# A decoder's first layer: weights loaded ahead of the mask, ternary weights made during attention, causal scores begun as the mask, ten steps for eleven

## The chip, the cores and the metric

The kernel runs on one core of a Trainium2 chip. The metric is device time in microseconds (us) of one execution, the median of several runs. A core has five engines with a queue of instructions each: PE (TensorE, matmuls and transposes; its weight loads are shown apart as PEld), DVE (VectorE), ACT (ScalarE), POOL (GpSimd) and SP (SyncE, which here only issues DMAs). DMAs are issued from the queues of SP, ACT and POOL, and each issuer has a DMA queue of its own, served by the same 16 DMA engines.

## The reference

A decoder of four layers, each of self-attention, cross-attention to a context and a feed-forward part (ffn), on 8 sequences of 128 tokens with 256 features, all in f32. The change touches layer 0 alone:

```python
x = x + _L0_attn_ref(_layernorm(x), Wq, bq, Wk, bk, Wv, bv, Wp, bp)      # 16 heads of 16, causal
x = x + _L0_xattn_ref(_layernorm(x), ctx_1024, pos, pos, Wq, Wkv, Wout, bout)  # 32 heads of 8
x = x + _L0_ffn_ref(_layernorm(x), gate_w, gate_b, val_w, val_b, out_w, out_b) # 1024 hidden
...
def bit_linear(x, w, b):                       # the three matmuls of layer 0's ffn
    gamma_x = clip(max(abs(x), axis=-1), 1e-05)
    x_dq = clip(round(x * 127 / gamma_x), -128, 127) * gamma_x / 127
    gamma_w = clip(mean(abs(w)), 1e-05)
    w_dq = clip(round(w / gamma_w), -1, 1) * gamma_w
    return einsum('bsd,hd->bsh', x_dq, w_dq) + b
```

So the ffn's weights become ternary (-1, 0 or 1 times the mean magnitude of the whole matrix), and each row of activations is rounded to 255 steps of its own largest magnitude. The ffn is `bit_linear(silu(bit_linear(x, gate)) * bit_linear(x, val), out)`.

## The kernel before, in words

Tokens lie on the 128 partitions, one sequence (128 tokens) at a time; x stays in SBUF for the whole kernel. Where a matmul needs features on partitions, PE transposes (`norm_turned`, L186 to L191). A planner puts the instructions of each stage in an order per engine by their dependences and due times; inside `manual_schedule` (`in_step`, L384) the order is the one written.

*Start* (`decoder`, from L2446; 0 to 25 us). SP loads the constants. ACT's queue loads x in two halves (L2459) and, behind them, the context cx (L2480), which PE transposes into ctxT first of all. POOL makes a table less_own_rows (L2498, a tensor_scalar of 16x2048) in a short-lived pool "start" and writes it to DRAM as less_own (L2501). A second short-lived pool "mask" holds the mask mu, loaded by a DMA on POOL's queue (L2510); DVE makes mb and anyk of it (L2513 to L2515). The pool wp0, in which the weights w, their rows r and the streamed blocks st have two buffers each (`weights` L101 and L107, `stream` L137), is opened after these two, in the place that they leave.

*Self-attention* (`l0_attn`, 25 to 130 us). PE makes Q, K (L46, into qT and kb) and V (into va) for all 1024 tokens. Meanwhile POOL adds the projection's bias to x (L184, 8 adds). Then a loop, by hand, over eight sequences, in which step t does parts of sequences t, t-1, ... with lags 0 to 3, so eleven steps. For a sequence: 16 score matmuls into the one buffer "sc" of four PSUM banks (L209); DVE adds the causal mask (L280, constant of 0 and -1e30) and copies into s in SBUF; DVE takes the row maxima (L285); POOL subtracts them (L286); ACT takes the exponentials in place (L301); PE turns the probabilities four times (L345), ACT copies each (L347), PE multiplies by the values; ACT copies the sum out (L367), PE turns it back (L375), DVE divides (L312, L316), PE projects, DVE adds to x (L195). At sequence 2 of `score` the kernel calls `clear_rows` (L1014): POOL issues one DMA of 8.4 MB that fills rows_in, a DRAM table which layer 1's ffn uses, with zeros.

*Cross-attention* (`l0_xattn`, 130 to 278 us): a prelude of projections and a rotary embedding, then a loop by hand of 16 units (two halves of the heads for each sequence), with four s buffers and four os buffers.

*ffn* (`l0_ffn`, 278 to 383 us). Front, to the first gate at 309.76: for each of three weights of 128x2048, DVE sums the magnitudes (L599), makes the mean (L602, L603, over a matmul with ones), and rounds it in three passes (L604 to L606) to bf16 wb. The loads of the first two lie in the two st buffers since the start of the kernel, and DVE made their sums at 32.80; the third is loaded when a buffer comes free. Then x is normalized (L618 to L624), the rows' maxima are taken (L632), xq is made in three passes (L640 to L642), and PE turns it (L648). Loop over eight sequences: gate and value matmuls in bf16, DVE scales and adds bias (L658, L663), ACT applies SiLU (L659), POOL multiplies (L664), DVE takes the row maximum (L667), rounds h in three passes (L673 to L675) to hq, PE turns it (L679), multiplies by the third weight, DVE adds to x (L683). Adding and subtracting the constant MAGIC = 1.5 * 2^23 rounds an f32 to an integer.

*Folds* (`folds`, L748 on): a generator of twelve pieces that make weights of later layers out of the inputs. A piece loads fold_vo on SP (L783, L784; two buffers), PE turns it (L769), ACT copies (L770), PE multiplies (L46), ACT copies out to fold_out (L775; two buffers) and SP writes that to DRAM (L776). Four pieces stand before the ffn's x work in the program, one in each step of the loop.

Of the kernel before, what the change touches and what calls it, by code (L numbers as in the profile page):

```python
# [8 lines left out]
F32 = mybir.dt.float32  # L9
BF16 = mybir.dt.bfloat16  # L10
# [187 lines left out]
def tok(b):  # L198
    return slice(b * S, (b + 1) * S)
# [24 lines left out]
def l0_attn(k):  # L224
# [7 lines left out]
    with k.tc.tile_pool(name="l0a", bufs=2) as wk_:  # L232
# [9 lines left out]
        for g in range(2):  # L242
            ts_ = slice(g * 512, (g + 1) * 512)
            for o in range(NC):
# [10 lines left out]
                )  # L255
        for b in range(B):
# [10 lines left out]
        caus = k.c[:, C_CAUS : C_CAUS + P].unsqueeze(1).to_broadcast([P, H, P])  # L267
        k.banks({"tr": 2, "po": 1, "o": 1})
        S_, PO, OS, PB, OB, PY = {}, {}, {}, {}, {}, {}
        act = nc.scalar.copy  # L270

        def score(b):
            if b == 2:
                clear_rows(k)
            psc = k.sct()
            for o in range(NC):
                scores(k, lambda r, n: psc[:, r, o * 256 : o * 256 + n], qT[:, o, tok(b)], kb[:, o, :, tok(b)])
            s = S_[b] = wk_.tile([P, 4, 4, P], F32, name="s", bufs=4)
            sv = s.rearrange("p r g t -> p (r g) t")
            nc.vector.tensor_tensor(sv, psc.rearrange("p r (g t) -> p (r g) t", t=P), caus, ALU.add)  # L280

        def less_max(b):
            sv = S_[b].rearrange("p r g t -> p (r g) t")
            mx = k.sm.tile([P, H], F32, name="mx")
            nc.vector.tensor_reduce(mx, sv, AX.X, ALU.max)  # L285
            nc.gpsimd.tensor_tensor(sv, sv, mx.unsqueeze(2).to_broadcast([P, H, P]), ALU.subtract)  # L286

        def values(b):
            po = PO[b] = k.pot()

            def use(g, pT):
                for r in range(4):
                    nc.tensor.matmul(
                        po[32 * r : 32 * r + 32, g, :], va[:, b, g, r, :], pT[:, r, :], start=True, stop=True
                    )

            round_about(k, wk_, lambda g: S_[b][:, :, g, :], [act] * 4, use)

        def exp(b):
            sf = S_[b].rearrange("p r g t -> p (r g t)")  # L300
            nc.scalar.activation(sf, sf, AF.Exp, scale=HD**-0.5)  # L301
# [21 lines left out]
        def project(b):  # L323
# [8 lines left out]
            (3, copied), (3, turn), (0, score), (3, divided), (0, less_max),  # L332
            (2, values), (1, exp), (3, project), (3, lambda b: k.add_x(b, PY[b])),
        )


def round_about(k, wk_, src, copies, use):


    done = {}  # L340
    for g in range(6):
        if g < 4:
            pt = k.trt()
            for r in range(4):
                k.nc.tensor.transpose(pt[:, r, :], src(g)[:, r, :], k.ident)  # L345
            done[g] = wk_.tile([P, 4, P], F32, name="pT", bufs=3)
            copies[g](done[g], pt)  # L347
        if g >= 2:
            use(g - 2, done[g - 2])
# [14 lines left out]
def back(k, wk_, po):  # L364

    os_ = wk_.tile([P, 4, P], F32, name="os", bufs=4)
    k.nc.scalar.copy(os_, po)  # L367
    return os_
# [19 lines left out]
def l0_xattn(k):  # L388
# [7 lines left out]
    with k.tc.tile_pool(name="l0x", bufs=2) as wk_, ExitStack() as inner:  # L396
# [104 lines left out]
        def score(u):  # L501
# [3 lines left out]
            s = S_[u] = wk_.tile([P, 4, 4, P], F32, name="s", bufs=4)  # L505
# [38 lines left out]
        def copied(b):  # L544
            OS[b] = back(k, wk_, PO[b])
# [36 lines left out]

def l0_ffn(k):
# [6 lines left out]
    with k.tc.tile_pool(name="l0f", bufs=2) as wk_:  # L590
        pieces = folds(k, wk_)
        wb = wk_.tile([P, 3, 2048], BF16, name="wb", bufs=1)
        gam = k.sm.tile([P, 3], F32, name="gam")
        rgam = k.sm.tile([P, 3], F32, name="rgam")
        part = k.sm.tile([P, 3], F32, name="part")
        for m in range(3):
            w = k.stream(a["p2"][m])[:, 0:2048]
            gm, rm = gam[:, m : m + 1], rgam[:, m : m + 1]
# [11 lines left out]
        for _ in range(4):  # L610
            next(pieces)
# [2125 lines left out]
```

## Time and profile before

| | us |
|---|---|
| median of three runs | 1948.71 |
| lowest and highest of them | 1945.85, 1960.44 |
| the profiled execution, its own time | 1957.12 |
| its span | 1955.3 |
| granted TensorE clock over the span | 0.939 |
| Q, K, V of layer 0 | 25.47 to 49.20 |
| layer 0's attention loop | 49.20 to 130.30 |
| its cross-attention, prelude and loop | 130.30 to 277.90 |
| its ffn, front and loop | 277.90 to 382.50 |

The profile is of one execution. Its page lists the busy time of each engine, the costliest groups of instructions (a line number is that of the kernel file, with output <- inputs, shape, count, busy time, mean of one in ns, and the idle time of the engine before them with what ended it), the chain of waits that ended last, and the DMA queues. A row of the timeline is: start, duration, engine, line, operation, output <- inputs, shape, count and, in brackets, how long its engine had been idle and what released it; "PEq", "SPq" and the like are the issue of a DMA by that engine's queue. A row of the DMA view is: queue, packets, MB, share of 16 engines' time; q1 is SP's queue, q10 ACT's, q0 POOL's. Some rows of the attention loop, for 49.2 to 130.3 us:

```profile
L286 POOL TENSOR_TENSOR s<-s,mx 128x2048 f32<-128x2048 f32 x8 | 28.9, 3611 | 47.0 <-DVE mx L285 33.6 <-ACT s L301 13.4
L280 DVE TENSOR_TENSOR s<-ps_sc,consts 128x2048 f32<-128x2048 f32 x8 | 18.3, 2287 | 11.8 <-PE ps_sc L209 11.8
L285 DVE TENSOR_REDUCE mx<-s 128x16 f32<-128x2048 f32 x8 | 18.2, 2280 | 0.2
L347 ACT COPY pT<-ps_tr 128x512 f32<-128x512 f32 x32 | 18.3, 587 | 26.9 <-PE ps_tr L345 26.9
```

DVE's two passes over a sequence's scores take 2.29 and 2.28, POOL's 3.61.

### The profile page before, as it was taken

Reading aid. Unit: us, or ns where it says so; the run is one execution under the profiler, and the core shown is the slowest. Engines: PE = TensorE matmul, PEld = TensorE weight load, DVE = VectorE, ACT = ScalarE, POOL = GpSimd, SP = SyncE. Lnnn points to the kernel's source line nnn. Section 1 sums busy time; section 2 is a strip of 40 time slices with the busy share of each in tenths; the row PEclk is TensorE's granted clock in tenths of the full one; section 3 lists DMA queues with packets and bytes.
Section 4 is the critical chain, followed back from the end, with each engine's and each line's share of the span. In section 5 each row is a group of like instructions: output and inputs, shape, how many; then the busy total and the mean of one; then the engine's idle time right before and its main releaser. Section 6 shows DMA issues by size and latency. Waiting matters only on the chain.

```text
span 1955.3 us, 25181 instructions
## 1 busy us (share of the span) xinstructions
PE 1717.8 (88%) x9471; PEld 1136.2 (58%) x9477; DVE 1203.0 (62%) x2374; ACT 1037.7 (53%) x1711; POOL 365.8 (19%) x359
## 2 busy tenths in 40 slices
PE   5776977667999986998788989999999997999999
PEld 3453655444666653664466545555555556888667
DVE  4766778856677752326756767677676775454423
ACT  2445854434667741225464377778777763343432
POOL 3543542201121222332002000000000001333200
PEclk9896988878999997998999999999999998999989
DMA  4600026305000022111001110101101004000000
GB/s 135 177 25 1 2 97 209 111 1 215 1 12 6 12 82 105 50 41 51 17 1 36 17 50 18 33 18 34 34 18 34 18 1 162 1 1 1 1 1 22
DMA packets 38970, 90.29 MB, mean 46 GB/s; under 512 B 6865, under 2 KB 19490, under 8 KB 37186
## 3 DMA queue, kind: packets, MB, share of 16 engines
q1 hardware_dynamic: 31266, 69.43, 10.4%
q0 software_dynamic: 5488, 17.67, 3.0%
q8 instruction: 76, 1.25, 0.3%
q10 hardware_dynamic: 2096, 1.57, 0.3%
q14 instruction: 44, 0.36, 0.1%
HBM read 67.15 MB, written 21.51 MB: 45 GB/s over the span
## 4 chain that ended last, share of the span: by engine, by line
PE 68%; DVE 14%; ACT 11%; issue 3%; POOL 2%; DMA 1%; ACTq 0%; DVEq 0%; SPq 0%; POOLq 0%
PE ps_xz L46 9%; PE ps_o L46 7%; PE ps_o L2077 6%; PE ps_o L848 5%; PE ps_mm L46 5%; PE ps_q L46 5%; PE ps_h L46 4%; PE ps_u L46 3%; PE ps_sc L46 3%; PE ps_y L46 2%; PE ps_ty L46 2%; PE ps_xz L1994 2%; DVE mx L511 2%; PE ps_ty L2015 2%; PE ps_sc L209 2%
## 5 line engine op out<-in xcount | busy, mean ns | idle before, releaser
L46 PE MATMUL ps_xz<-xnT,wxz 128*128 128x512 f32 x512 | 237.1, 607 | 0.3 <-ACT ee L1997 0.3
L46 PEld LDWEIGHTS ps_xz<-xnT,wxz 128*128 128x128 f32 x512 | 93.3, 192 | 103.9 <-issue 101.9
L1974 DVE SCALAR_TENSOR_TENSOR xc<-pad,w,xc 128x1024 f32<-128x1024 f32 x96 | 123.1, 1282 | 30.5 <-ACT xc L1968 28.7
L2077 PE MATMUL ps_o<-wo,yg 128*128 128x256 f32 x512 | 128.0, 395 | 1.5 <-DVE yg L2056 1.5
L848 PE MATMUL ps_o<-wvo,uT 128*128 128x256 f32 x512 | 122.6, 383 | 0.0
L848 PEld LDWEIGHTS ps_o<-wvo,uT 128*128 128x128 f32 x512 | 98.5, 193 | 40.7 <-issue 30.3
L1997 ACT ACTIVATE ee<-ps_xz,sgn 128x512 f32<-128x512 f32 x128 | 87.1, 689 | 60.2 <-PE ps_xz L1994 60.2
L2077 PEld LDWEIGHTS ps_o<-wo,yg 128*128 128x128 f32 x512 | 93.5, 192 | 25.4 <-issue 12.9
L2017 DVE TENSOR_TENSOR dtx<-ps_ty,dt 128x512 f32<-128x512 f32 x64 | 41.4, 687 | 90.1 <-PE ps_ty L2015 89.9
L2369 POOL MEMSET gb<- 128x160 f32 x1 | 0.2, 231 | 504.1 <-PE ps_ty L46 504.1
L46 PE MATMUL ps_h<-moe,xT 128*128 x184 | 85.1, 606 | 0.9 <-DVE xT L1244 0.8
L2007 DVE TENSOR_TENSOR ee<-ee,gT 128x2048 f32<-128x2048 f32 x32 | 73.2, 2288 | 8.9 <-ACT ee L2003 8.9
L46 PE MATMUL ps_u<-pT,cx 128*128 128x512 f32 x128 | 70.0, 629 | 6.8 <-ACT pT L831 6.7
L947 ACT ACTIVATE s<-ps_sc,mx,rqs 128x128 f32<-128x128 f32 x128 | 48.1, 456 | 49.5 <-DVE rs_t L129 48.0
L2003 ACT ACTIVATE ee<-ee,sgn 128x1024 f32<-128x1024 f32 x64 | 73.0, 1145 | 0.2
L955 POOL TENSOR_TENSOR s<-s,sums 128x512 f32<-128x512 f32 x32 | 33.3, 1040 | 207.7 <-DVE sums L954 66.6
L512 POOL TENSOR_TENSOR s<-s,mx 128x2048 f32<-128x2048 f32 x16 | 57.8, 3610 | 53.6 <-DVE mx L511 53.6
L1258 DVE TENSOR_TENSOR h<-ps_h,sl 128x512 f32<-128x512 f32 x23 | 15.9, 692 | 82.2 <-PE ps_h L46 82.2
L46 PEld LDWEIGHTS ps_q<-xnT,wqk 128*128 128x128 f32 x512 | 64.3, 199 | 2.8 <-DVE xnT L62 1.0
L46 PE MATMUL ps_q<-xnT,wqk 128*128 128x128 f32 x512 | 64.8, 282 | 0.6 <-DVE xnT L62 0.6
L46 PE MATMUL ps_ty<-ee,dtx 128*64 128x128 f32 x1024 | 63.0, 276 | 2.3 <-DVE ee L2007 2.2
L358 PE MATMUL ps_tr<-consts,s 128*128 128x128 f32 x384 | 55.7, 290 | 8.4 <-ACT s L1726 3.3
(599 smaller groups left out, 4038.3 us busy)
## 6 DMA issues: line engine op xcount, KB each, us to landing
moe<-in_p SPq DMA_DIRECT2D x24, 512.0 KB
rows_in<-zero_rows POOLq DMA_DIRECT2D x1, 8385.0 KB, 34.4
wxz<-in_p9s SPq DMA_DIRECT2D x32, 256.0 KB
fold_vo<-in_p SPq DMA_DIRECT2D x8, 512.0 KB
wvo<-fold_out SPq DMA_DIRECT2D x16, 256.0 KB
wvo<-wvo SPq DMA_DIRECT2D x2, 2048.0 KB
wo<-in_p9s SPq DMA_DIRECT2D x16, 256.0 KB
st<-in_p SPq DMA_DIRECT2D x3, 1024.0 KB
```

Source lines behind the costliest of these rows:

```text
L46: nc.tensor.matmul(out, lhsT, rhs, start=(i == 0), stop=(i == len(pairs) - 1))
L209: k.nc.tensor.matmul(psc(r, n), q[rows], rhs, start=True, stop=True)
L358: k.nc.tensor.transpose(pt[:, r, :], src(g)[:, r, :], k.ident)
L512: nc.gpsimd.tensor_tensor(sv, sv, mx.unsqueeze(2).to_broadcast([P, 16, P]), ALU.subtract)
L848: k.nc.tensor.matmul(self.po[b], uT[:, j, :], self.wvo[:, 4 * hg + j, :], start=hg + j == 0, stop=hg + j == 6)
L947: nc.scalar.activation(s[:, j, :], psc[:, j, :], AF.Exp, scale=rs[:, j : j + 1], bias=mx[:, j : j + 1])
L1974: nc.vector.scalar_tensor_tensor(XC[n], (PAD[n] if n in PAD else pads[n % 2])[:, :, t : t + S], cw[:, n, t : t + 1], XC[n], ALU.mult, ALU.add)
L1997: nc.scalar.activation(e, pm, AF.Relu, scale=sgn[:, at : at + 1])
L2003: nc.scalar.activation(EE[n][:, h], EE[n][:, h], AF.Exp, scale=sgn[:, at : at + 1])
L2007: nc.vector.tensor_tensor(EE[n], EE[n], gT.unsqueeze(1).to_broadcast([P, 2, B, S]), ALU.mult)
L2017: nc.vector.tensor_tensor(DTX[n][:, bs], pt.rearrange("p (b h d) -> p b h d", b=4, d=HD), dt_[:, bs, 2 * n : 2 * n + 2].unsqueeze(3).to_br ...
L2077: nc.tensor.matmul(PO[b // 2][:, b % 2 * D : (b % 2 + 1) * D], YG[n][:, tok(b)], WO[n // 2][:, n % 2, :], start=False, stop=n == 31 and b ...
```

## The change

1. *Start.* The pools "start" and "mask" lie at the other end of SBUF (`side="right"`), so wp0 no longer takes their place. less_own_rows is made by ACT. ACT loads its table for exp and ln first.
2. *Ternary weights.* A new function `ternary` makes one weight; the first two are made in `l0_attn`, after K's second half, with the two clamping passes on POOL and the rounding pass on ACT. The third is made in the ffn, with the clamping on DVE and the rounding on ACT; its load is issued when a buffer of the first two is free. wb moves into the pool wp0.
3. *Causal scores.* Per sequence PE first writes the mask into each of the four banks (a bf16 matmul of the identity with a bf16 copy of the mask, start without stop) and the scores add to it. DVE takes the maxima from PSUM and subtracts them from PSUM into s, by halves (two of the four head groups); POOL's subtraction is gone; ACT's exponential goes by halves too. Lags run from 0 to 2, so ten steps.
4. *Cross-attention.* s has three buffers for four, os two for four.
5. *ffn.* x is normalized, scaled, rounded and turned by four sequences at a time, with `norm_rows` in place of the Sqrt, and in two passes for three (the clamps, which nothing reaches beyond rounding, are left out). The fold pieces come after it in the program. In the loop, hq is made by one pass on DVE and one on ACT, for three on DVE.

In the order that the planner gives the changed kernel: w, r, and both st loads are issued on SP directly behind the constants. On POOL, clear_rows' DMA stands directly behind the first memset of va, ahead of less_own's and mu's DMAs; mu's DMA waits for less_own, and behind it follow seven of the eight x adds and the four ternary passes. The loop's `score` of sequence 2 still calls `clear_rows`, but POOL has no instruction of the loop before it. On DVE, in the first step, the order is: maxima and subtraction of sequence 0's first half, mb and anyk, its second half, the sum over the third ternary weight, sequence 1. The third weight's load waits for ACT's rounding of the first, which stands behind the exponential of sequence 0's first half.

```diff
@@ -253,6 +253,9 @@
                 nc.vector.tensor_scalar(
                     kb[:, o, 1, ts_], pm, k.m16[:, 1:2], bkm[:, o, 1:2], ALU.mult, ALU.add
                 )
+            if g:
+                for m in range(2):
+                    ternary(k, m, nc.gpsimd)
-        caus = k.c[:, C_CAUS : C_CAUS + P].unsqueeze(1).to_broadcast([P, H, P])
+        caus = wk_.tile([P, P], BF16, name="caus", bufs=1)
+        nc.vector.tensor_copy(caus, k.c[:, C_CAUS : C_CAUS + P])
...
         def score(b):
             if b == 2:
                 clear_rows(k)
-            psc = k.sct()
+
+            psc = SC[b] = k.sct()
+            for r in range(4):
+                nc.tensor.matmul(
+                    psc[:, r, :], k.ident_b, caus.unsqueeze(1).to_broadcast([P, 4, P]), start=True, stop=False
+                )
             for o in range(NC):
-                scores(k, lambda r, n: psc[:, r, o * 256 : o * 256 + n], qT[:, o, tok(b)], kb[:, o, :, tok(b)])
-            s = S_[b] = wk_.tile([P, 4, 4, P], F32, name="s", bufs=4)
-            sv = s.rearrange("p r g t -> p (r g) t")
-            nc.vector.tensor_tensor(sv, psc.rearrange("p r (g t) -> p (r g) t", t=P), caus, ALU.add)
-
-        def less_max(b):
-            sv = S_[b].rearrange("p r g t -> p (r g) t")
-            mx = k.sm.tile([P, H], F32, name="mx")
-            nc.vector.tensor_reduce(mx, sv, AX.X, ALU.max)
-            nc.gpsimd.tensor_tensor(sv, sv, mx.unsqueeze(2).to_broadcast([P, H, P]), ALU.subtract)
...
+            S_[b] = wk_.tile([P, 4, 4, P], F32, name="s", bufs=3)
+            MX[b] = k.sm.tile([P, 4, 4], F32, name="mx")
+
+        def less_max(o):
+            def f(b):
+                js = slice(2 * o, 2 * o + 2)
+                bank = SC[b].rearrange("p r (g t) -> p r g t", t=P)[:, :, js, :]
+                mx = MX[b][:, :, js]
+                nc.vector.tensor_reduce(mx, bank, AX.X, ALU.max)
+                nc.vector.tensor_tensor(
+                    S_[b][:, :, js, :], bank, mx.unsqueeze(3).to_broadcast([P, 4, 2, P]), ALU.subtract
+                )
+
+            return f
+
+        def exp(o):
+            def f(b):
+                sf = S_[b][:, :, 2 * o : 2 * o + 2, :]
+                nc.scalar.activation(sf, sf, AF.Exp, scale=HD**-0.5)
+
+            return f
+
+        def turn_p(some):
+            def f(b):
+                for g in some:
+                    pt = k.trt()
+                    for r in range(4):
+                        nc.tensor.transpose(pt[:, r, :], S_[b][:, r, g, :], k.ident)
+                    PT[b, g] = wk_.tile([P, 4, P], F32, name="pT", bufs=4)
+                    nc.scalar.copy(PT[b, g], pt)
+
+            return f
+
+        def values(some):
+            def f(b):
+                if some[0] == 0:
+                    PO[b] = k.pot()
+                for g in some:
+                    pT = PT.pop((b, g))
+                    for r in range(4):
+                        nc.tensor.matmul(
+                            PO[b][32 * r : 32 * r + 32, g, :], va[:, b, g, r, :], pT[:, r, :], start=True, stop=True
+                        )
+
+            return f
...
         in_step(
             k, B,
-            (3, copied), (3, turn), (0, score), (3, divided), (0, less_max),
-            (2, values), (1, exp), (3, project), (3, lambda b: k.add_x(b, PY[b])),
+            (0, score), (2, turn), (1, turn_p((0, 1))), (0, less_max(0)), (2, divided), (0, exp(0)),
+            (1, turn_p((2,))), (1, values((0,))), (1, turn_p((3,))), (1, values((1,))), (2, project),
+            (0, less_max(1)), (1, values((2, 3))), (2, lambda b: k.add_x(b, PY[b])), (1, copied), (0, exp(1)),
         )
...
+def back(k, wk_, po, bufs=4):
+
+    os_ = wk_.tile([P, 4, P], F32, name="os", bufs=bufs)
     k.nc.scalar.copy(os_, po)
     return os_
...
-            s = S_[u] = wk_.tile([P, 4, 4, P], F32, name="s", bufs=4)
...
-            OS[b] = back(k, wk_, PO[b])
...
+def ternary(k, m, eng):
+
+    nc = k.nc
+    if m == 0:
+        k.wb = k.wp.tile([P, 3, 2048], BF16, tag="wb", name="wb", bufs=1)
+        k.gam, k.rgam, k.part = (k.sm.tile([P, 3], F32, name=n, bufs=1) for n in ("gam", "rgam", "part"))
+    w = k.stream(k.a["p2"][m])[:, 0:2048]
+    gm, rm, part = (t[:, m : m + 1] for t in (k.gam, k.rgam, k.part))
+    nc.vector.tensor_reduce(part, w, AX.X, ALU.add, apply_absolute_value=True)
+    pg = k.ot((P, 1))
+    mm(nc, pg, [(k.ones, part)])
+    nc.vector.tensor_scalar(gm, pg, 1.0 / (1024 * D), 1e-05, ALU.mult, ALU.max)
+    nc.vector.reciprocal(rm, gm)
+    eng.tensor_scalar(w, w, rm, 1.0, ALU.mult, ALU.min)
+    eng.tensor_scalar(w, w, -1.0, MAGIC, ALU.max, ALU.add)
+    nc.scalar.activation(k.wb[:, m, :], w, AF.Copy, bias=-MAGIC)
+
...
-        for m in range(3):
-            w = k.stream(a["p2"][m])[:, 0:2048]
...
-            nc.vector.reciprocal(rm, gm)
-            nc.vector.tensor_scalar(w, w, rm, 1.0, ALU.mult, ALU.min)
-            nc.vector.tensor_scalar(w, w, -1.0, MAGIC, ALU.max, ALU.add)
-            nc.vector.tensor_scalar(wb[:, m, :], w, MAGIC, None, ALU.subtract)
+        for m in range(2):
+            if l0_attn not in LAYERS:
+                ternary(k, m, nc.vector)
+        wb, gam = k.wb, k.gam
...
-        for _ in range(4):
-            next(pieces)
...
-        xn = k.xp.tile([P, B, D], F32, name="xn", bufs=1)
-        for b in range(B):
-            nc.vector.tensor_scalar(
-                xn[:, b, :], x[:, b, :], mv[:, b, 0:1], rstd[:, b : b + 1], ALU.subtract, ALU.mult
-            )
-            nc.gpsimd.tensor_tensor(x[:, b, :], x[:, b, :], obias, ALU.add)
...
-        nc.vector.tensor_reduce(gx, xn, AX.X, ALU.max, apply_absolute_value=True)
...
-        for b in range(B):
-            nc.vector.tensor_scalar(xn[:, b, :], xn[:, b, :], sx[:, b : b + 1], 127.0, ALU.mult, ALU.min)
-            nc.vector.tensor_scalar(xn[:, b, :], xn[:, b, :], -128.0, MAGIC, ALU.max, ALU.add)
-            nc.vector.tensor_scalar(xq[:, b, :], xn[:, b, :], MAGIC, None, ALU.subtract)
         for g in range(2):
+            k.norm_rows(g)
+            gs = slice(4 * g, 4 * g + 4)
+            xn = k.xn[:, gs, :]
+            nc.vector.tensor_reduce(gx[:, gs], xn, AX.X, ALU.max, apply_absolute_value=True)
+            nc.vector.tensor_scalar(gx[:, gs], gx[:, gs], 1e-05, None, ALU.max)
+            nc.vector.reciprocal(sx[:, gs], gx[:, gs])
+            nc.vector.tensor_scalar(sx[:, gs], sx[:, gs], 127.0, None, ALU.mult)
+            for b in range(4 * g, 4 * g + 4):
+                nc.vector.tensor_scalar(k.xn[:, b, :], k.xn[:, b, :], sx[:, b : b + 1], MAGIC, ALU.mult, ALU.add)
+            nc.vector.tensor_scalar(xq[:, gs, :], xn, MAGIC, None, ALU.subtract)
+            for of, m in ((dg, 0), (dv, 1)):
+                nc.vector.tensor_scalar(of[:, gs], gx[:, gs], gam[:, m : m + 1], 1.0 / 127.0, ALU.mult, ALU.mult)
             for c in range(NC):
                 pt = k.trt((P, 4, P), BF16)
                 for j in range(4):
                     nc.tensor.transpose(pt[:, j, :], xq[:, 4 * g + j, c * P : (c + 1) * P], k.ident_b)
                 k.evac(xqT[:, c, g * 512 : (g + 1) * 512], pt.rearrange("p j t -> p (j t)"))
+        k.normed = 0
+        ternary(k, 2, nc.vector)
+        for _ in range(4):
+            next(pieces)
+        for b in range(B):
+            nc.gpsimd.tensor_tensor(x[:, b, :], x[:, b, :], obias, ALU.add)
         for b in range(B):
...
             hq = wk_.tile([P, FF], BF16, name="hq")
-            nc.vector.tensor_scalar(h, h, sh, 127.0, ALU.mult, ALU.min)
-            nc.vector.tensor_scalar(h, h, -128.0, MAGIC, ALU.max, ALU.add)
-            nc.vector.tensor_scalar(hq, h, MAGIC, None, ALU.subtract)
+            nc.vector.tensor_scalar(h, h, sh, MAGIC, ALU.mult, ALU.add)
+            nc.scalar.activation(hq, h, AF.Copy, bias=-MAGIC)
...
+    k.exp_table()
...
-    with tc.tile_pool(name="start", bufs=1) as start:
+    with tc.tile_pool(name="start", bufs=1, side="right") as start:
         rows = start.tile([2 * B, 2 * B, S], BF16, name="less_own_rows")
-        nc.gpsimd.tensor_scalar(
-            rows, k.c[0 : 2 * B, C_ID : C_ID + 2 * B].unsqueeze(2).to_broadcast([2 * B, 2 * B, S]), -1.0, None, ALU.mult
+        nc.scalar.activation(
+            rows, k.c[0 : 2 * B, C_ID : C_ID + 2 * B].unsqueeze(2).to_broadcast([2 * B, 2 * B, S]), AF.Copy, scale=-1.0
         )
         nc.gpsimd.dma_start(k.less_own, rows)
...
-    with tc.tile_pool(name="mask", bufs=1) as start:
+    with tc.tile_pool(name="mask", bufs=1, side="right") as start:
         mu = start.tile([P, B, S], U8, name="mu")
```

## The prediction

> **What bounds the kernel now.** I read the chain of waits of the page first, for the engines that carry the end; then busy time by stage, since only layer 0 (0 to 383 us of 1955) is touched; then the timeline of the start, the chain across the first ffn, and the DMA queues in short windows.
>
> ```profile
> PE 68%; DVE 14%; ACT 11%; issue 3%; POOL 2%; DMA 1%; ACTq 0%; DVEq 0%; SPq 0%; POOLq 0%
> ```
> Over the whole kernel PE carries the end. The touched stages differ (columns: stretch, length, busy time of PE, weight loads, DVE, ACT, POOL, then PE clock, DMA share, GB/s):
>
> ```profile
> 25.47:49.20 23.73, 23.25 (x68) 12.48 (x68) 10.91 (x21) 5.86 (x8) 5.50 (x8) 1.00 0.33 132
> 49.20:130.30 81.10, 59.04 (x580) 39.41 (x580) 54.23 (x72) 38.35 (x51) 34.78 (x13) 0.85 0.37 107
> 277.90:309.70 31.80, 19.80 (x81) 14.73 (x83) 28.37 (x60) 9.59 (x18) 5.90 (x8) 0.72 0.81 266
> 309.70:382.50 72.80, 51.48 (x320) 35.10 (x322) 61.81 (x128) 33.80 (x56) 21.83 (x16) 0.87 0.46 162
> ```
> Q, K and V (row 1) are PE's. The attention loop (row 2) is full on no engine. The ffn's front and loop (rows 3, 4) are DVE's: 89% and 85%.
>
> ```profile
> 9.35 1.94 PE L219 MATMUL ps_tr<-consts,cx 128*128 128x128 f32 x8 [9.35 <-DMA cx<-in_ctx]
> 13.20 0.62 POOL L2510 DMA_DIRECT2D mu<-in_mask_BxS_bf  x1 [1.94 <-DMA less_own<-less_own_rows]
> 20.21 0.33 SPq L101 DMA_DIRECT2D w<-in_p  x1
> 25.47 16.06 PE L46 MATMUL ps_mm<-xnT,w 128*128 128x512 f32 x32 [6.62 <-DMA w<-in_p]
> 63.15 2.95 POOL L1014 DMA_DIRECT2D rows_in<-zero_rows  x1
> ```
> PE's first work is the transposes of cx. The first weights are issued only at 20.21, after the mask work, and PE idles 6.62 for them. The 8.4 MB write of rows_in goes out at 63.15, with x, cx and all first weights long landed.
>
> ```profile
> q1 hardware_dynamic: 41, 0.15, 80.1%
> q10 hardware_dynamic: 32, 0.03, 18.5%
> ...
> q10 hardware_dynamic: 53, 0.05, 69.2%
> q1 hardware_dynamic: 59, 0.00, 16.2%
> ```
> These are two short windows (3.0 to 3.5, 5.0 to 5.2; packets, MB, share of 16 engines). SP's queue q1 carries 3.7 KB packets of consts in the first and 8-byte packets in the second, ACT's queue q10 1 KB packets of x in both. Each time the counts are nearly equal: the queues take turns by packet, not by byte.
>
> ```profile
> q0 software_dynamic: 744, 3.07, 104.2%
> ```
> Ten us of rows_in alone (80 to 90): 4.1 KB packets, 10/744 = 0.0134 us each.
>
> ```profile
> 283.74 2.36 DVE wb L606 x2
> 286.25 5.14 DVE xn L624 x8
> 291.41 2.29 DVE gx L632
> 293.69 2.20 DVE part L599
> ...
> 297.73 3.79 PE ps_mm L46 x8
> ...
> 303.05 3.97 DMA fold_vo<-in_p
> ```
> The chain across the ffn's front begins on DVE but ends in the folds: their matmuls and their loads.
>
> **The change, part by part.** The profiled execution took 1957.12 (span 1955.3), 8.4 above the median 1948.71; the sum is made on the span and added to the median.
>
> *Start.* With its own side for the short-lived tiles, w no longer waits for the mask work: its issue goes from 20.21 to about 1.5, its 5.22 transfer (20.21 to 25.43) is done by about 7. Alone this would start Q, K, V up to 6.6 earlier, x's norm being then the limit. But the causal subtraction leaves POOL, so nothing on POOL stands ahead of clear_rows any more: the program order has its DMA right after the va memset (4.8 here). First data came 3.2 after issue at 63.15, so rows_in flows from about 8, beside x and cx.
>
> x is 1024 packets of 1 KB, cx 1024 of 512 B behind them on one queue. Prices per packet on 16 engines: x 0.0027 and cx 0.0017 (608 cx packets took 1.0 us), rows_in 0.0134, st and w 0.019 to 0.022 (43 packets of w in 1 us). Consts, w and r (384 packets) go ahead until 7.7, about 340 x packets between them. Then three queues: SP still has st, st, w, r, 512 packets, 256 x 0.019 + 128 x 0.015 + 128 x 0.003 = 7.2; with 512 of rows_in (6.9) and 512 of x (1.4) this ends at 23. 172 more pairs of x: 26. Then 1024 pairs of cx and rows_in at 0.0151: 15.4, so cx lands at about 42. Bounds: 14, if bytes are shared evenly, and 48, if cx ends with rows_in's 2095 packets; the two-window row is nearest, so 42. PE's queue starts with cx, and x's norm, the xnT transposes and Q, K, V stand behind it. From cx to Q is then transposes 1.94, copy 0.6, xn 0.5, transposes 1.94, copy 0.6, hops 0.4 = 6: Q starts at 48.5, that is 23 later than 25.47, and the first scores at 48.5 + 23.7 = 72.2 against 49.2.
>
> The Trainium skill, "DMA: Bandwidth & Descriptors", section "Queues, rings and completion order", says that each DMA engine goes round the queues it has work for and switches only after a whole packet. That speaks against this change: by it a small-packet queue beside a 4 KB one gets the sum above, and by even bytes cx would land near 14 and the sum would be the rival's 1947. The two windows agree with the page; none shows it for POOL's queue.
>
> *Mask.* less_own and mu are queued behind rows_in on POOL's queue and mu waits for less_own: mu lands at about 51 (rows_in ends near 47 here, 42 + 387 packets x 0.0134; two waits of 2). Its reader, DVE's cast of mb, stands between the halves of sequence 0, not due before 74: hidden. Eight x adds (5.5) and four ternary steps on POOL follow, to about 66. One step of 128x2048 lies between 1.76 (the 128x4096 memset took 3.52) and 5.38 (less_own_rows); the subtraction with two inputs took 3.61, a 128x256 copy 0.40. I take 2.5. Cover: ACT's rounding is not due before 79, so even 5.38 is hidden here.
>
> *Third ternary weight.* A new wait: its st buffer is free when ACT has rounded the first weight, which stands behind exp of sequence 0's first half. Sequence 0's DVE work ends about 72.2 + 2.7 (scores) + 7.4 (two halves of 2 x 1.2, mb 2.6) = 82.3; ACT rounds at 79.1 to 81; SP issues at 81.1; 5.2 for 1 MB, as w took: 86.3; the sum over it on DVE 2.27: 88.6. All DVE work of sequence 1 is queued behind. In before sequence 1 began at 54.92: +33.7.
>
> *Attention loop.* A step was 7.66 (x adds at 77.06, 84.77, 92.43, 100.09). Now the bank is held until both halves are subtracted, so PE's scores and DVE follow each other: DVE two maxima and two subtractions 4.5, rec, ob, x 1.2; PE 16 scores 1.15, 4 mask matmuls at 0.24 (the ffn's bf16 128x512 row) 0.95; hops 0.5: 8.3. Bounds: 7.0, if half of PE hides, and 9.6, if ACT's half exponentials add to it. From sequence 1 to the last x add: 6 x 8.3 + 4 (norm of half the rows, as now) + tail 15 (two steps of lag at PE's and ACT's 7.5) = 68.8, against 130.3 - 54.9 = 75.4: -6.6. Attention ends 33.7 - 6.6 = +27 late.
>
> *Cross-attention.* Fewer buffers (4 to 3, 4 to 2): the reuse comes three units and two sequences later and is free by then; half of the ffn's norm moves in, some 4 us of DVE, which is busy 75 of 114 here. Zero; without that cover +4.
>
> *ffn front.* Ternary leaves DVE (7.4 us of rows L604 to L606, 2.3 of L599 and the third weight), rows are quantized in two passes instead of three. DVE from the last x add to the first gate falls from 31.9 to about 13. But five fold pieces still stand ahead of the first gate matmul on PE, each with its load of about 4 and two buffers: at about 5 apiece, 26.4. So -5.5; bounds -3 and -18 (DVE alone).
>
> *ffn loop.* Each of 8 steps loses 1.36 of DVE (two passes of 0.68; ACT takes one at about 1.0, from its 0.58 for 512 columns): 10.9 of DVE's 61.8. PE waited 6.1 for hq and DVE 6.5 for POOL's h, which stay: I take -7.5, bounds -4 and -11.
>
> **Sum:** 27 - 5.5 - 7.5 = +14: 1971 in the profiled execution's terms, 1948.7 + 14 = 1963 as a median.
>
> **Rivals.** *The queues share more evenly* (for: POOL's queue was never seen beside another; against: both windows). cx lands near 14, the first scores start near 44, but mu still lands after rows_in, then 5.2 of adds and two POOL steps: rounding near 63, sum over the third weight done at 72.8. Attention ends 72.8 + 68.8 = 141.6, +11; less 13: 1947.
>
> *rows_in holds neither cx nor mu.* Then only the third weight's wait is left: 44 + 16.4 = 60, attention ends at 129, -1.5; with -13, 1934; with the folds' faster pace too (front -12), 1928.
>
> *The other side: attention steps serial.* If the exponentials' release of banks and the transposes on PE fall between scores, a step takes 9.6: 7 x 1.3 (the six, and the last sequence's own) = +9, 1972. For it: row 2 has no full engine, so waits set the step. It decides from 9.05 a step on (1968 - 1963 over 7).
>
> **Numbers.** About 1% is what a measurement of this kernel can tell from no change: 1929 to 1968. Forecast 0.60 at 1963 (its own range 1952 to 1976 from cx at 30 to 48, the steps and the front; a third of it above 1968); serial steps 0.15, nearly all above 1968; even sharing 0.15 at 1947; nothing held 0.10 at 1934, half of it below 1929, and a little of the even case too. Slower 0.20 + 0.14 = 0.34; faster 0.07; within 0.59. Range 1936 to 1979.
>
> **What would show it.** Transposes of cx near 42 with cx's DMA as releaser; scores of sequence 0 near 72; a DVE gap before the sum over the third weight, sequence 1 near 88; x adds 8.3 apart; first gate 26 after the last x add of cross-attention, PE waiting for fold_vo. Wrong if cx lands before 20, or if the ffn gives 20.

## The result, and the profile after

The changed kernel took 1981.1 us (median of four runs, 1973.9 to 1982.7) against 1950.8 for the kernel before on the same chip: a ratio of 1.0142, 95% interval 1.0095 to 1.0189. On the first median of 1948.7 that is 1976. The forecast was 1963 within 1936 to 1979; it called a time above 1968 slower and gave that 0.34, against 0.59 for a time within 1%. The profiled execution spans 1979.9, against 1955.3.

Nearly all of it lies in layer 0. The table gives start times in the two traces; the difference is how late the changed kernel then was. "First gate" is the start of DVE's first scaling of gate sums (L658 before, L681 after). The rest of the execution (from the first add to x in layer 1's self-attention) took 1538.2 in the changed kernel and 1537.3 in the one before.

| start of | before | after | late | late in the forecast |
|---|---|---|---|---|
| cx's transposes on PE | 9.35 | 34.96 | 25.6 | 33 |
| Q's matmuls | 25.47 | 40.86 | 15.4 | 23 |
| sequence 1's work on DVE | 54.92 | 88.52 | 33.6 | 33.7 |
| last x add, self-attention | 130.27 | 153.31 | 23.0 | 27 |
| last x add, cross-attention | 277.89 | 309.16 | 31.3 | 27 |
| first gate of the ffn | 309.76 | 338.23 | 28.5 | 21.5 |
| last x add of the ffn | 382.54 | 407.66 | 25.1 | 14 |
| first x add, layer 1 | 418.00 | 441.69 | 23.7 | 14 |

The page of the changed kernel still has PE carry the end (62%); the shares sum to 81%, since the chain there goes back only to 372.7, near the end of layer 0's ffn. The stages (stretch, length, busy time of PE, weight loads, DVE, ACT, POOL, clock, DMA share, GB/s):

```profile
40.86:64.54 23.68, 23.65 (x75) 13.70 (x75) 17.43 (x28) 6.45 (x9) 12.57 (x10) 1.00 0.26 72
64.54:153.73 89.19, 61.91 (x616) 39.26 (x615) 66.09 (x92) 42.86 (x62) 25.85 (x9) 0.89 0.04 13
309.60:338.20 28.60, 19.41 (x76) 14.65 (x78) 10.57 (x28) 11.17 (x20) 2.98 (x4) 0.75 0.79 258
338.20:408.00 69.80, 48.89 (x321) 33.98 (x325) 52.79 (x114) 43.46 (x66) 20.81 (x16) 0.94 0.45 154
```

Q, K, V are as long as before. The attention loop is 8 longer though it has a step less. In the ffn's front DVE's work fell from 28.4 to 10.6, and the front only from 31.8 to 28.6.

The timeline of the start, in the changed kernel:

```profile
4.73 3.10 POOL L1036 DMA_DIRECT2D rows_in<-zero_rows  x1
...
17.73 0.43 DVE L155 BATCH_NORM_STATS2 ln<-x 128x6 f32<-128x256 f32 x1 [10.29 <-DMA x<-in_x]
...
34.96 1.94 PE L219 MATMUL ps_tr<-consts,cx 128*128 128x128 f32 x8 [34.96 <-DMA cx<-in_ctx]
...
40.86 1.92 PE L46 MATMUL ps_mm<-xnT,w 128*128 128x512 f32 x2
...
47.73 0.61 POOL L2533 DMA_DIRECT2D mu<-in_mask_BxS_bf  x1 [9.13 <-DMA less_own<-less_own_rows]
```

And the DMA queues in its stretch from 15 to 25 (queue, packets, MB, share):

```profile
q0 software_dynamic: 509, 2.10, 53.6%
q1 hardware_dynamic: 500, 1.57, 39.8%
q10 hardware_dynamic: 512, 0.28, 9.9%
```

Three queues whose packets were of 4.1, 3.1 and 0.5 KB in the mean (MB by packets) moved 509, 500 and 512 of them: turns by packet, POOL's queue included. DVE waited 10.3 for x's second half, and cx landed only at 35.

The first step of the loop, with POOL's passes over the ternary weights:

```profile
66.71 1.23 DVE L302 TENSOR_REDUCE mx<-ps_sc 128x8 f32<-128x1024 f32 x1 [1.48 <-PE ps_sc L287]
67.85 4.69 DVE L2536 CAST mb<-mu 128x1024 f32<-128x1024 uint8 x1
71.97 15.03 POOL L620 TENSOR_SCALAR st<-st 128x2048 f32<-128x2048 f32 x2
72.47 1.20 DVE L303 TENSOR_TENSOR s<-ps_sc,mx 128x1024 f32<-128x1024 f32 x1
...
73.59 1.20 DVE L2537 TENSOR_REDUCE anyk<-mb 128x8 f32<-128x1024 f32 x1
...
75.85 4.22 DVE L2538 TENSOR_SCALAR mb<-mb 128x1024 f32<-128x1024 f32 x1
79.55 1.91 ACT L621 ACTIVATE wb<-st 128x2048 bf16<-128x2048 f32 x1 [4.79 <-POOL st L620]
...
86.32 2.29 DVE L614 TENSOR_REDUCE part<-st 128x1 f32<-128x2048 f32 x1 [5.13 <-DMA st<-in_p]
...
88.52 1.22 DVE L302 TENSOR_REDUCE mx<-ps_sc 128x8 f32<-128x1024 f32 x1
```

A POOL pass takes 7.2 to 7.5. DVE's cast of mb, 0.68 in the kernel before, takes 4.69 and ends at 72.5, just after POOL's pass ended at 72.0; the later pass over mb (L2538, 4.22 for 0.69) ends just after POOL's next one. The reduction between them keeps its 1.20. In the trace the cast stands ahead of the subtraction of sequence 0's first half, not behind it, so that subtraction starts only at 72.47.

The Trainium skill, "SBUF — State Buffer", section "Who interferes with whom", has the rule: VectorE and GpSimd share a pair of ports that one instruction holds whole, and casts and tensor_scalars on SBUF can need it while a tensor_reduce does not. These rows agree with it; it speaks against moving long passes to POOL, and the forecast did not use it.

Last, the unit of cross-attention in which the ffn's norm of the first half now stands:

```profile
260.23 0.41 DVE L195 TENSOR_TENSOR x<-ps_tr,x 128x256 f32<-128x256 f32 x1
...
260.40 3.61 POOL L535 TENSOR_TENSOR s<-s,mx 128x2048 f32<-128x2048 f32 x1 [3.01 <-DVE mx L534]
...
261.20 1.28 ACT L125 ACT_TABLE_LOAD   x1
261.36 2.67 DVE L158 TENSOR_SCALAR ln_var<-ln_mv 128x4 f32<-128x4 f32 x1
...
264.29 1.28 ACT L126 ACT_TABLE_LOAD   x1
...
266.42 2.20 DVE L165 TENSOR_SCALAR xn<-x,ln_mv,ln 128x256 f32<-128x256 f32 x4
...
270.53 1.11 PE L381 MATMUL ps_tr<-consts,s 128*128 128x128 f32 x4 [7.56 <-DVE pT L383]
...
281.64 0.42 DVE L195 TENSOR_TENSOR x<-ps_tr,x 128x256 f32<-128x256 f32 x1
```

The x adds of the loop stand 12.2 apart, these two 21.4. DVE and ACT do the norm's steps in turn, each waiting for the other, while PE waits 7.56 for a copy that is queued behind them. Some 2.5 of it is POOL's again: DVE's L158 on 128x4, 0.15 at the start of the kernel, takes 2.67 here and ends with POOL's subtraction (264.0).

### The profile page after: what moved, and what is told of

The parts are those of the page before. It is cut to its first block, busy times and chain, and to the rows that moved or that the text cites. A ratio compares the mean times of both kernels' runs of the same rounds, so it can differ in the third digit from the quotient of the medians.

```text
span 1979.9 us, 25266 instructions
## 1 busy us (share of the span) xinstructions
PE 1715.8 (87%) x9503; PEld 1132.8 (57%) x9509; DVE 1197.6 (60%) x2367; ACT 1058.2 (53%) x1737; POOL 360.9 (18%) x354
## 3 DMA queue, kind: packets, MB, share of 16 engines
q1 hardware_dynamic: 31266, 69.43, 10.3%
## 4 chain that ended last, share of the span: by engine, by line
PE 62%; ACT 9%; DVE 8%; issue 2%; POOL 0%; DMA 0%; DVEq 0%; ACTq 0%; POOLq 0%
PE ps_xz L46 9%; PE ps_o L2099 6%; PE ps_o L46 6%; PE ps_o L870 5%; PE ps_q L46 5%; PE ps_h L46 4%; PE ps_mm L46 4%; PE ps_u L46 3%; PE ps_sc L46 3%; PE ps_y L46 2%; PE ps_ty L46 2%; PE ps_xz L2016 2%; PE ps_ty L2037 2%; ACT sq L2091 1%; PE ps_tr L948 1%
## 5 line engine op out<-in xcount | busy, mean ns | idle before, releaser
L977 POOL TENSOR_TENSOR s<-s,sums 128x512 f32<-128x512 f32 x32 | 33.3, 1041 | 207.9 <-DVE sums L976 66.3
L46 PE MATMUL ps_q<-xnT,wqk 128*128 128x128 f32 x512 | 64.8, 282 | 0.6 <-DVE xnT L62 0.6
```

What stands on the lines that cost most here:

```text
L46: nc.tensor.matmul(out, lhsT, rhs, start=(i == 0), stop=(i == len(pairs) - 1))
```

## The experiments

All ratios are to the kernel before on the same chip, over at least four runs. Start times are from the traces. "First x add" is layer 1's, 418.0 before and 441.7 after. Executions whose start is the changed kernel's reach Q up to 1.2 earlier than its own trace (39.7 to 40.9); where it matters this is taken off.

**1. The write of rows_in moved.** `clear_rows` is called in cross-attention's loop:

```diff
-            if b == 2:          # l0_attn, score
-                clear_rows(k)
...
+            if u == 2:          # l0_xattn, score
+                clear_rows(k)
```

> The changed kernel with the 8.4 MB write of rows_in issued in the cross-attention's loop (at its unit 2) and nothing else changed. Theory (the write, put first on POOL's queue, starves cx): cx lands at 18 to 20 instead of 35 (the weights' packets on SP's queue still take turns with x), Q starts near 25 instead of 40.9. Then POOL's four ternary passes at 7.3 each and the load of the third ternary weight bind: first maxima of sequence 1 near 77 instead of 88.5, time 1981 - 11 = 1970 (1966 to 1974). Rival (the first weights' own packets on SP's queue are what delays cx, the write only follows): cx still lands after 30 and the time stays within 1978 to 1983.

Measured: cx's transposes at 20.92, Q at 28.41, ratio 1.0104 (1.0071 to 1.0136); first x add 433.1.

```profile
20.92 1.94 PE L219 MATMUL ps_tr<-consts,cx 128*128 128x128 f32 x8 [20.92 <-DMA cx<-in_ctx]
...
23.24 4.54 DVE L165 TENSOR_SCALAR xn<-x,ln_mv,ln 128x256 f32<-128x256 f32 x6
...
45.35 14.32 POOL L618 TENSOR_SCALAR st<-st,rgam 128x2048 f32<-128x2048 f32 x2 [14.57 <-DVE rgam L617]
59.66 14.18 POOL L619 TENSOR_SCALAR st<-st 128x2048 f32<-128x2048 f32 x2
...
73.74 2.29 DVE L613 TENSOR_REDUCE part<-st 128x1 f32<-128x2048 f32 x1 [20.84 <-DMA st<-in_p]
```

The write costs Q 12.5 of its 15.4. The other 2.9 are not the weights' packets alone: the pools by themselves (experiment 6) make Q 1.2 later, and from cx to Q this run takes 7.5 instead of 5.9, with six xn passes of DVE taking 4.54 instead of 2.44 while POOL adds to x beside them. Of the 12.5 self-attention keeps 4.9 (last x add 148.43), since DVE then waits 20.84 for the third weight behind POOL's passes: the next wait, as the theory had it. The planner's order on DVE is another one here: the sum over the third weight now stands ahead of sequence 0's maxima (75.94). Sequence 1 came at 84.8, not 77: its scores need the one bank, and so the end of sequence 0's subtractions.

**2. No ternary weight in attention.** All three are made in the ffn's front:

```diff
-            if g:
-                for m in range(2):
-                    ternary(k, m, nc.gpsimd)
...
-            if l0_attn not in LAYERS:
-                ternary(k, m, nc.vector)
+            ternary(k, m, nc.vector)
```

> The changed kernel with all three ternary weights made in the ffn's front on DVE and ACT, none in attention. Theory (sequence 1 waits for the third weight's load, that for ACT's rounding of the first, that for POOL's passes of 7.3): the sum over the third weight leaves the first step, mb's two passes take 0.7 each instead of 4.7 and 4.2, sequence 1 begins at 74 to 76 instead of 88.5; the ffn's front takes the passes behind the folds, 0 to 2 longer: 1981 - 12 = 1969 (1966 to 1972). Rival (sequence 1 is late only by the late start): sequence 1 begins after 85 and the time stays, or rises by 3 to 5 for the passes in the front.

Measured: sequence 1 at 76.5, last x add of self-attention 140.86 (12.5 earlier; Q was 1.2 earlier in this execution, so 11.3 gained), ratio 1.0092 (1.0072 to 1.0113); first x add 436.8.

```profile
66.69 0.68 DVE L2532 CAST mb<-mu 128x1024 f32<-128x1024 uint8 x1
...
70.68 0.68 DVE L2534 TENSOR_SCALAR mb<-mb 128x1024 f32<-128x1024 f32 x1
...
76.52 1.22 DVE L299 TENSOR_REDUCE mx<-ps_sc 128x8 f32<-128x1024 f32 x1 [4.03 <-PE ps_sc L284]
```

mb's passes are back to 0.68 each without POOL beside them. Cross-attention gets 0.9 longer, the front 3.1 (32.2), the loop 2.0, layer 1's start 1.5: 7.5 of the 12.5 is given back by layer 1's first x add.

**3. The third weight alone.** Its sum is put behind self-attention; the first two are made on POOL as in the change:

```diff
...
-        ternary(k, 2, nc.vector)
+        with k.tc.issue_after(k.att_added.ins):   # the last x add of l0_attn
+            ternary(k, 2, nc.vector)
```

> The changed kernel with the sum over the third ternary weight issued on DVE behind self-attention's last x add, and nothing else. It parts the 12 us by which sequence 1 began earlier with no ternary work in attention into the wait for the third weight and the wait of DVE for POOL. Theory (DVE's passes over mb end only when POOL's ternary passes do: two waits of 4.0 and 3.5; the third weight is what holds sequence 1 after that): mb still takes 4.7 and 4.2, sequence 0's DVE work still ends near 81, sequence 1's first maxima stand near 85 instead of 88.5, last x add of self-attention at 149 to 150.5 instead of 153.3, 3 below the changed kernel, ratio to before 1.012 (1.010 to 1.014). Rival 1 (the third weight alone makes the delay): sequence 1 at 78 or earlier. Rival 2 (POOL and DVE alone, the third weight hides beside them): sequence 1 stays after 87.5, no gain.

Measured: sequence 1 at 83.41 (Q was 0.9 earlier in this execution, so 4.2 gained), but the last x add at 151.68 (0.7 gained); ratio 1.0133 (1.0110 to 1.0156).

```profile
70.48 15.02 POOL L621 TENSOR_SCALAR st<-st 128x2048 f32<-128x2048 f32 x2
...
85.53 1.91 ACT L622 ACTIVATE wb<-st 128x2048 bf16<-128x2048 f32 x1 [5.56 <-POOL st L621]
...
87.34 1.04 ACT L312 ACTIVATE s<-s 128x1024 f32<-128x1024 f32 x1
...
95.23 1.22 DVE L302 TENSOR_REDUCE mx<-ps_sc 128x8 f32<-128x1024 f32 x1 [6.95 <-PE ps_sc L287]
```

The theory fell on the end and held on the start. What sequence 1 gained is lost in the next step: ACT's rounding of the second weight waits for POOL's last pass, and sequence 0's second exponential is queued behind it at 87.34. POOL's passes hold the loop in three ways (DVE's passes, ACT's queue, the third weight's load); taking one away leaves the others.

**4. The ffn's norm behind cross-attention.**

```diff
...
-            k.norm_rows(g)
+            with k.tc.issue_after(k.added.ins):       # the last x add
+                k.norm_rows(g)
```

> The changed kernel with the ffn's norm of both halves issued on DVE only behind the last x add of the cross-attention. Theory (the norm of the first half, put between the units with its two loads of an ACT table, costs one step of the cross-attention 9.2): all x adds of sequences 1 to 6 stand 12.1 to 12.2 apart, last one at 300 instead of 309.2; the front gets 1 to 4 longer, since fold pieces bind it: 1981 - 6.5 = 1974.5 (1972 to 1977). Rival 1 (the step is long by the three s buffers or by POOL's bias adds): one gap stays at 20 or more, time 1980 to 1986. Rival 2 (the work only moves): the front gets 9 longer, time 1981.

Measured: x adds of sequences 1 to 5 12.2 apart, the last of cross-attention 145.7 after self-attention's instead of 155.9; the front 29.1, as in the change; ratio 1.0104 (1.0083 to 1.0125), first x add 433.0. The norm inside the loop costs 10.2 and gives the front nothing, so something else binds the front. Without it cross-attention is 1.9 shorter than in the kernel before (147.6).

**5. The folds behind the ffn's loop.**

```diff
-        for _ in range(4):
-            next(pieces)
...
             nc.vector.scalar_tensor_tensor(x[:, b, :], py, gh, x[:, b, :], ALU.mult, ALU.add)
+        for _ in pieces:
+            pass
```

> The changed kernel with the four fold pieces that stand ahead of the first gate made after the ffn's loop, and nothing else. Theory (in the changed kernel PE waits in the ffn's front for the loads and copies of the folds, while DVE is busy 10.6 of 28.6): from the last x add of cross-attention to the first gate 14 to 18 instead of 29; some of it is given back behind the loop: 8 below the changed kernel, ratio to before 1.010 (1.007 to 1.012). Rival (the norm's and the rounding's chain through ACT sets the front): front above 24, ratio 1.013 or more.

Measured: ratio 1.0019 (1.0004 to 1.0034), the front 8.6, first x add 420.1. Three times the gain that I expected. What PE waited for in the front of the changed kernel (in all, times, longest), and the two stages of this experiment:

```profile
PE ps_mm L46 <- DMA fold_vo<-in_p: 5.7, 2, 3.2
PE ps_mm L46 <- ACT fold_vT L792: 2.1, 3, 0.7
```

```profile
308.20:316.90 8.70, 6.41 (x26) 4.57 (x25) 8.17 (x19) 4.42 (x7) 2.98 (x4) 0.55 0.74 256
316.90:376.50 59.60, 50.10 (x336) 34.46 (x334) 52.33 (x118) 40.55 (x66) 20.97 (x16) 1.00 0.64 215
```

Front 29.1 to 8.6 and loop 69.4 to 59.1, while 10.1 came back between the ffn's last x add and layer 1's first (34.0 to 44.1). The front was the folds': PE's own work in it fell from 19.4 to 6.4, and the two waits above from 7.8 to 0.7. That the loop, too, got 10.3 shorter I had not foreseen. In the loop DVE's waits for POOL's h fell from 11.2 to 4.7 and PE's for hq from 8.3 to 1.1, and PE is busy 84% of it instead of 70%; but the eight pieces left in it are other ones, and why they fit better was not tried. The granted clock (1.00 here, 0.94 in the changed kernel) cannot be the main reason: in experiment 7 the same edit takes the loop from 69.6 to 60.7 at 0.96 and 0.95. The same edit in the kernel before was not tried.

**6. Parts of the change alone, in the kernel before.** The two pools on the other side alone; the same with x and cx on SP's queue ahead of the weights (`nc.sync.dma_start` for `nc.scalar.dma_start`); and the new attention loop alone, with rows_in written in cross-attention.

> The kernel before with the two short-lived pools on the other side alone, so that the first weights are loaded at once. Theory (packets of the weights delay x and cx by as much as the weights come earlier): w lands near 7, cx at 17 to 20 instead of 9.35, Q starts at 24 to 26 instead of 25.47: within 2 of before. Rival (the start alone is worth what PE idled for w): Q starts near 19, time 5 to 7 below before.

> The kernel before with the two short-lived pools on the other side, and x and cx on SP's queue ahead of the weights; nothing else of the change. Theory: Q starts at 17 to 19 instead of 25.47 (26.7 with the pools alone) and the gain stays through layer 0: 7 to 8 below before, ratio 0.996. Rival (a wait further on takes it back): last x add of the ffn within 3 of before's 382.5, ratio 0.998 or above.

> The kernel before with the new attention loop alone (scores begun as the mask, subtraction on DVE by halves, ten steps), rows_in written in the cross-attention's loop so that it meets no load. Theory (a step of 7.8 against 7.66, but one step and part of the tail fewer): from the first maxima to the last x add 72 to 73 instead of 79.9, last x add at 123 to 124 instead of 130.3, 6 below before, ratio 0.997 (0.995 to 0.999). Rival (the bank, held until the second subtraction, makes the loop slower): last x add after 131, ratio above 1.000.

Measured: the pools alone cx at 20.51, Q at 26.70, ratio 0.9977 (0.9958 to 0.9996). Weights issued 19 earlier (1.2 instead of 20.21) bring Q nothing, since cx comes 11 later. The ratio is 4.5 below before, where the theory had at most 2 and the trace shows 2.7 at layer 1's first x add; its interval reaches from 0.8 to 8, and the difference is not explained. With one queue, cx at 9.64, Q at 18.96, last x add of the ffn 369.59 in the trace, ratio 0.9984 (0.9967 to 1.0001): the trace shows layer 0 to be 13 shorter, but it is of the fastest of ten runs (1940.5, clock 0.946); their mean shows 3, at a granted clock of 0.941 against 0.943. That gap is not explained, and the time came out as the rival had it. The loop alone: last x add 124.57 for 130.27, ratio 0.9972 (0.9958 to 0.9985): about as expected. The loop, with rows_in out of it, is a gain; what the write's new place alone is worth in the kernel before was not tried.

**7. Repairs together.** "three" has 1, 2 and 4; "three_q" has x and cx on SP's queue as well; "three_q_folds" has 5 as well.

> The changed kernel with all three repairs: rows_in written in the cross-attention's loop, all three ternary weights made in the ffn, the ffn's norm issued behind the last x add. Theory (three separate losses that add up): Q near 28, last x add of self-attention near 128.5 (before 130.3), of cross-attention near 274, first gate 33 later at 308 since the folds bind the front, last x add of the ffn at 379 (before 382.5): 3 below before, ratio 0.998 (0.995 to 1.001). Rival (they cover the same wait, so that repairing one uncovers the next): last x add of the ffn at 388 or more, ratio 1.003 or above.

> The kernel 'three' with x and cx loaded on SP's queue, ahead of w, r and the st blocks, instead of on ACT's queue beside them. Theory (small packets lose to large ones only when they stand on two queues): x's second half lands near 7.5, cx near 9 to 10, w near 11 to 13, Q starts at 17 to 19 instead of 28: 10 below 'three', 13 below before, ratio 0.993 (0.990 to 0.996). Rival (another load or the norm sets Q): Q after 24, no gain over 'three'.

> The kernel 'three_q' with the four fold pieces that stood ahead of the first gate made after the ffn's loop. Theory (the folds, their loads and PE, set the ffn's front, so its shorter DVE work showed little): from the last x add of the cross-attention to the first gate 16 to 20 instead of 29 to 33. What the four pieces cost after the loop is open: between 0 and 20; I expect 8 below 'three_q', ratio 0.989. Rival (DVE's or ACT's own work sets the front): front still above 26, time that of 'three_q' or more.

| | Q | last x add: self-, cross-attention | first gate | first x add, layer 1 | ratio |
|---|---|---|---|---|---|
| three | 28.78 | 126.54, 272.35 | 304.86 | 410.28 | 0.9996 (0.9979 to 1.0014) |
| three_q | 13.29 | 118.55, 265.29 | 297.76 | 403.26 | 0.9934 (0.9913 to 0.9955) |
| three_q_folds | 13.08 | 118.70, 264.49 | 289.60 | 393.33 | 0.9897 (0.9867 to 0.9928) |

The times of "three" and "three_q" came out as expected: the losses add up (singly the repairs took 0.0038, 0.0050 and 0.0038 off the ratio, together 0.0146). In "three_q" Q came 4 earlier than expected, but a wait for mu behind it took that back. On one queue the small packets cost nothing (cx at 9.62, before at 9.35):

```profile
9.62 1.94 PE L219 MATMUL ps_tr<-consts,cx 128*128 128x128 f32 x8 [9.62 <-DMA cx<-in_ctx]
...
13.29 2.18 PE L46 MATMUL ps_mm<-xnT,w 128*128 128x512 f32 x4
...
20.98 3.44 PE L46 MATMUL ps_mm<-xnT,w 128*128 128x512 f32 x4 [5.52 <-DVE xnT L62]
```

(The wait of 5.52 at 20.98 is DVE's, whose cast of mb waits for mu until 18.36.) In "three_q_folds" the front fell to 25.1 only, not to 16 to 20: there the three ternary weights, all in the front, keep DVE busy 22.75 of 25.1, and PE waits 11.5 for xq.

**8. A version with all repairs.** As "three_q_folds", with the first two ternary weights made on DVE in attention, the third summed behind it, and mu on ACT's queue in a place of its own.

```diff
-                    ternary(k, m, nc.gpsimd)
+                    ternary(k, m, nc.vector)
...
-        mu = start.tile([P, B, S], U8, name="mu")
-        nc.gpsimd.dma_start(
+        mu = const.tile([P, B, S], U8, name="mu")
+        nc.scalar.dma_start(
```

> All repairs in one: rows_in in the cross-attention's loop, x and cx on SP's queue ahead of the weights, mu on ACT's queue in a place of its own, the first two ternary weights clamped on DVE while V is made, the third summed behind self-attention, the ffn's norm behind the last x add, four fold pieces behind the ffn's loop. Theory (each loss was taken separately): Q at 13 to 17, last x add of self-attention near 116, of cross-attention near 263, first gate 15 to 19 later near 280 (289.6 in three_q_folds), ratio to before 0.985 (0.981 to 0.989). Rival (the DVE passes among V's copies hold V and the first scores): last x add of self-attention after 121, ratio 0.989 or more.

Measured: ratio 0.9872 (0.9845 to 0.9900), the lowest of all, its interval overlapping "three_q_folds"; first x add 392.72. The front is 18.5 as expected. But self-attention ends at 122.86, not 116. PE waits 4.30 in V for DVE, whose passes over the two weights stand among V's copies, as the rival said:

```profile
40.52 4.73 PE L46 MATMUL ps_o<-w,xnT 128*128 128x256 f32 x13 [4.30 <-DVE va L264]
```

Against "three_q_folds", whose self-attention ends at 118.70, that is not a loss by itself: from Q to the first maxima both take about 33 (32.8 and 33.3), since there DVE's wait for mu, as in "three_q", takes as much. What is lost is that Q starts 3.9 later (16.93), behind a cx that lands at 11.82, with mu's load beside it on ACT's queue; mu's new place was not tried alone. Of the 6.6 that the front gains over "three_q_folds", 4.2 is lost up to self-attention's end.

## Why the prediction was right or wrong

The direction, and the mechanism that it put first, were right; the sum came out 11 short of the trace (+14 against +25.1 at the ffn's end), by errors of both signs. The 14 of the forecast is half of the 27 that the medians show, so that 1976 still lies in the range owes much to the range's width.

- *Start.* Right in kind: cx starved behind rows_in. The size was too large, +15.4 on Q instead of +23: no packet of rows_in moved before 12, while the forecast had it flow from 8. Experiment 1 shows the write to be 12.5 of it.
- *mu hidden.* Its load was hidden (landed by 51); its cast was not, for the reason in the next point.
- *POOL's four passes.* The step that failed. The forecast took 2.5 each, with 5.38 as the upper bound; they took 7.2 to 7.5. "Even 5.38 is hidden here" left out DVE's 4.0 and 3.5 of waiting and ACT's queue. Sequence 1 still began at 88.52 (forecast 88.6): the start 7.6 earlier than forecast, POOL's passes as much later. Two errors cancelled; the number alone would have passed for a proof.
- *The third weight.* It was late as forecast (sum at 86.3), but it was not what held the loop alone: without its wait self-attention gained 0.7 (experiment 3), without all ternary work 11.3 (experiment 2).
- *Attention loop.* A step took 7.85 (x adds at 110.34, 118.19, 126.05), between the bounds of 7.0 and 9.6, for 8.3; from sequence 1 to the last x add 64.8 went by for 68.8. The rival of serial steps did not occur.
- *Cross-attention at zero.* Wrong: +8.3. The cover was named (DVE busy 75 of 114) and its price without it put at 4; in a loop in written order, DVE's spare time is no cover for a chain that goes through ACT and back, and that stops 2.5 beside POOL's subtraction on the way. Experiment 4: 10.2 for the norm, of which the rest of the stage got 1.9 back.
- *ffn.* Front -2.8 for -5.5, loop -3.4 for -7.5. The folds were named as what binds the front, and experiment 5 shows that; they were priced too low, and in the loop they were not counted at all. There DVE's work fell by 9.0 (10.9 in the sum), but of the waits "which stay" DVE's for POOL's h grew from 6.5 to 11.2 and PE's for hq from 6.1 to 8.3.

## What to carry to other kernels

Loads on several queues took turns by packet here (509, 500 and 512 in 10 us), so a small-packet load that the first matmul needs belongs ahead of the large ones on the same queue (cx at 9.6 instead of 21), and a bulk write must be held behind something until those have landed. When work is moved to an engine, ask which instructions of that engine's neighbours stop beside it and which are queued behind its results, not only whether the engine is free. When a stage's busiest engine is relieved, look for the wait that ends second: here folds that PE did ahead of its own work gave back 1.2% once moved, of the 1.4% that the whole change had lost.

## What was not expected of the hardware

A two-step tensor_scalar of 128x2048 in f32 took 7.16 on POOL (experiment 1) and 1.28 on DVE (experiment 8), a factor of 5.6. DVE's cast and tensor_scalar of mb on SBUF beside it ended only with POOL's instruction; its reductions and its operations from PSUM did not wait (a subtraction from PSUM kept 1.20). A tensor_tensor of two 128x1 inputs in SBUF waited too: 4.98, from 48.24, beside POOL's seven adds to x, for 0.13 in the kernel before. The rows_in write brought its first packets 7 us after its issue here, 3.2 in the kernel before; why is open.
